# One padded table for the position terms, a pinned order in the scan's last chunk, the state turned by halves, and the last spectral rows in two loads

## The chip, the cores and the metric

The kernel runs on one core of a Trainium2 chip. What counts is the device time of one execution in microseconds (us). Three executions of the kernel before took 3838.72, 3837.66 and 3835.54 us; their median is 3837.66 us. A further execution, with the hardware profiler on, gives the profile from which everything else is read.

## The reference

The input is one image of 48x48 positions with 768 channels, in float32. Four layers follow each other:

```
x = L0(x)   # attention with relative position terms, then an MLP
x = L1(x)   # spectral layer: rfft2, block MLP per frequency, softshrink, irfft2, + x
x = L2(x)   # scan: 12 rounds of a depthwise 3x3 convolution on a state
x = L3(x)   # spectral layer as L1, other weights
```

In layer 0, with 12 heads of 64 channels, the scores get two terms which depend on the query and on the distance of the two positions:

```
coords = arange(H)[:, None] - arange(H)[None, :] + (H - 1)
Rh = rel_pos_h[coords];  Rw = rel_pos_w[coords]          # rel_pos_*: (95, 64)
rel_h = einsum('bhwc,hkc->bhwk', q, Rh)
rel_w = einsum('bhwc,wkc->bhwk', q, Rw)
attn  = softmax(attn + rel_h[..., :, None] + rel_w[..., None, :])
```

For one row (or column) of queries the factor is thus a window of 48 columns of the same table of 95 columns, shifted by one from row to row. In layer 2, `rope` turns pairs of channels by an angle:

```
for i in range(12):
    inj  = rope(silu(x @ W_B + ...), theta * (i + 1)) * silu(x @ W_X + b_X)
    H    = alpha * (conv3x3(H) + conv_b) + [gamma *] inj [+ (1 - gamma) * alpha * prev]
    prev = inj
out = silu((rope(C, theta * 12) * H) @ W_out + b_out)
```

In layer 3 the inverse transform ends with the sum over the 25 kept column frequencies, real and imaginary parts, for each row of the image; the layer's input is added.

## The kernel before, in words

A Python function writes the program; a scheduler then places the instructions of each engine, and tile pools decide when a buffer is free. `V` is VectorE (DVE), `nc.scalar` is ScalarE (ACT), `GP` is GpSimd (POOL), `nc.tensor` is TensorE (PE), and most loads and stores are issued on SyncE (SP, `nc.sync`). A float32 matmul shows as two records of PE with a weight load each. The stages stand in time like this: query, key and value products (`qkv_phase`) to 479 us and their tail to 512, attention to 1690, projection to 1832, MLP to 2840, first spectral layer to 3060, projections of the scan to 3232, scan rounds 3244 to 3487, its output product to 3598, and the last spectral layer to the end.

**Position terms (`position_terms` in `qkv_phase`).** The tokens are worked on in three blocks `sb` of 768. For each block there are 24 steps, 12 `rel_h` (L415) and 12 `rel_w` (L401). A step makes four positions. For each it multiplies the queries of a pair of heads (128 rows, 64 to a head) with a block-diagonal matrix of 128x96: two copies of the window, one for each head, zeros elsewhere. These matrices are made on the host (`relD`) and loaded by `tables` (L376 to L380), 192 KB to a step, into four buffers, up to three steps ahead. The result, 96 rows in one PSUM tile, is split into three bf16 parts by `split` (L366 to L374: two copies on ACT, two subtractions on DVE) and stored at the end of each set (`store`, L390). `advance` runs one step. `between` calls it after the value products (L164), and `q_and_k` calls it between the query and key products (L295), so that the steps lie singly among full 128x128 products; what is left over follows at the end, where a matmul on the maxima (`bound`, L475) also decides which form of attention runs. `ahead(1)` issues the first loads of attention.

**Attention**, not touched, runs per round a score product on two 64x128 tiles (L559), the position terms added as a bf16 product of 120 rows (L567) and the product with the values on two 128x64 tiles (L588).

**Scan, first part.** The tokens come in 8 chunks (`q`, 0 to 7), on 112 partitions. For each chunk three products of PE (L1094) make injection `g`, `x`, angle `th`, `al` and `ga`; DVE adds the bias (L1096); ACT takes Silu and Sigmoid; `sincos` makes sine and cosine of the angle and of 12 times it; `turn` (L1279, six operations of DVE) turns `g` by the angle into `i0`; H, the first state, is `i0 + ac` (L1142). After this come the sums `s0` and `s1` for the rounds, from `u = by_gamma(...)` (ACT, L1119) at L1148 to L1154. **Rounds:** eight groups of eight channels, 11 rounds, 88 groups. A group is 32 matmuls (L1183: two tiles of 128x48 each, accumulated) into one of four PSUM tiles `c0` to `c3`, two operations of DVE (L1185, L1187), a product on POOL (L1191), a copy on ACT (L1192) and one more DVE operation (L1203). In the last round the state is multiplied with the turned C instead (L1209, into `s`; the last group on DVE, the others on POOL). **Output:** `hg` holds 24 position pairs with 256 channels. For each two pairs four transposes (L1254: two pairs, two halves `j` of the channels), a copy on ACT (L1256) and the output product (L1263, two halves of the channels accumulated).

**Last spectral layer.** `spectrum_mix` runs its items (two halves of the channels, five groups `kc` of five column frequencies, four channel blocks) through four stages; the last, `s_ifft_h` (L1503), fills `us`, which is stored to `yu` with the group's last block (L1510). The final part reads the rows of `yu` back: `load` takes one of the six row groups `g` of a half (L1524, all 112 rows, 672 KB, four buffers), and `back` multiplies them with `iw` (L1682), adds the input on DVE (L1684) and stores the output (L1688). `beside` places loads and products of half 0 during the mix; half 1 is loaded after the mix.

## Time and profile before

| what | us |
|---|---|
| median of three executions | 3837.66 |
| profiled execution, its own time | 3841.45 |
| its span, first to last instruction | 3839.7 |
| rh, L415 MATMUL: 288 records of 352 ns mean | 55.8 busy |
| rw, L401 MATMUL: 288 records of 264 ns mean | 32.1 busy |
| c, L1183 MATMUL: 5632 records of 247 ns mean | 242.2 busy |

The mean granted clock of TensorE is 0.986 of full speed. A row of the waits names an instruction that kept PE idle, what released it, the time in total, how often, and the longest. "issue" stands for a wait which the profile can't put down to anything. Busy times of PE overlap, because matmuls are pipelined; the time a matmul takes in the stream is the distance from its start to the next one's. A row of the timeline has the start in us from the span's first instruction, the length in us, engine, line, operation, output and inputs, the size of the tile of the array (rows*columns), the form of the operands, and how many such instructions the row stands for.

### The profile page before, as it was taken

The numbers are of one execution on the slowest core, as the hardware profiler recorded it, in microseconds if no ns is written. First come the engines' busy times: TensorE is split into PE (matmuls) and PEld (weight loads), VectorE is DVE, ScalarE is ACT, GpSimd is POOL, SyncE is SP. The second block draws the span as 40 slices with busy tenths as digits, with TensorE's granted clock in tenths as the row PEclk, the third lists the DMA queues.
The fourth block names the chain that finished last, engine by engine and source line by source line (L and its number), as shares of the span: only waits on it lengthen the run. The fifth ranks groups of instructions, "written<-read, shape, count | busy, mean of one in ns | idle before, by whom it ended". The sixth has DMA issues, their size and how long they took to land.

```text
span 3839.7 us, 54414 instructions
## 1 busy us (share of the span) xinstructions
PE 3727.7 (97%) x22018; PEld 2255.4 (59%) x22018; DVE 2057.3 (54%) x3184; ACT 1142.8 (30%) x1908; POOL 656.5 (17%) x498
## 2 busy tenths in 40 slices
PE   7999979999999999999999999999999998999998
PEld 4666544444444444445555555555568876996685
DVE  6655456666666666555524332323325567995455
ACT  1323234444444444420310120012013356222341
POOL 3101001111111111015000000000013311981131
PEclk9999989999999999999999999999999999999999
DMA  7656563333232322124434534443454312112345
GB/s 254 211 193 194 178 184 119 113 107 128 84 112 75 115 74 91 42 71 139 151 104 136 173 107 121 133 137 104 125 166 105 108 36 93 40 33 73 97 114 155
DMA packets 266762, 460.43 MB, mean 120 GB/s; under 512 B 32941, under 2 KB 219301, under 8 KB 260007
## 3 DMA queue, kind: packets, MB, share of 16 engines
q1 hardware_dynamic: 256695, 435.93, 37.0%
q10 hardware_dynamic: 9808, 20.94, 1.5%
q8 instruction: 175, 2.87, 0.3%
q14 instruction: 84, 0.69, 0.1%
HBM read 318.49 MB, written 138.31 MB: 119 GB/s over the span
## 4 chain that ended last, share of the span: by engine, by line
PE 93%; DVE 2%; DMA 2%; issue 1%; ACT 1%; POOL 1%; SPq 0%; DVEq 0%; ACTq 0%; POOLq 0%
PE p L867 13%; PE p L930 12%; PE s L559 12%; PE av L588 12%; PE c L1183 6%; PE s L567 6%; PE qk L295 6%; PE c L1094 4%; PE v L164 3%; PE pj L164 2%; PE f_z L1489 2%; PE f_z L1488 2%; PE f_x L1453 2%; PE so L1263 2%; PE f_u L1503 2%; PE rh L415 1%
## 5 line engine op out<-in xcount | busy, mean ns | idle before, releaser
L577 DVE TENSOR_TENSOR acc<-acc,p 128x768 f32<-128x768 f32 x576 | 584.1, 1014 | 355.1 <-ACT p L569 317.1
L569 ACT ACTIVATE p<-s 128x768 f32<-128x768 f32 x648 | 478.6, 812 | 693.7 <-PE s L567 581.2
L930 PE MATMUL p<-w,h 128*128 128x384 f32 x1512 | 492.7, 486 | 0.0
L559 PE MATMUL s<-qt,kv 64*128 64x384 f32 x2592 | 478.5, 501 | 9.9 <-ACT p L569 7.7
L588 PE MATMUL av<-p,kv 128*64 128x384 f32 x2592 | 464.5, 493 | 0.0
L930 PEld LDWEIGHTS p<-w,h 128*128 128x128 f32 x1512 | 286.1, 190 | 196.9
L559 PEld LDWEIGHTS s<-qt,kv 64*128 64x128 f32 x2592 | 233.1, 187 | 250.6 <-ACT p L569 116.3
L588 PEld LDWEIGHTS av<-p,kv 128*64 128x64 f32 x2592 | 170.0, 136 | 225.2 <-issue 215.2
L867 PE MATMUL p<-x2nT,w 128*128 128x384 f32 x864 | 294.2, 490 | 3.4 <-issue 3.4
L295 PE MATMUL qk<-xnT,wqk 128*128 128x384 f32 x756 | 251.8, 490 | 5.3 <-DMA wqk<-wqk_d 5.3
L1183 PE MATMUL c<-H,bands 128*48 128x96 f32 x5632 | 242.2, 247 | 12.4 <-issue 12.4
L567 PE MATMUL s<-bt,oneh 120*128 120x384 bf16 x1296 | 249.1, 329 | 0.0
L1183 PEld LDWEIGHTS c<-H,bands 128*48 128x48 f32 x5632 | 234.6, 123 | 20.2 <-issue 12.7
L867 PEld LDWEIGHTS p<-x2nT,w 128*128 128x128 f32 x864 | 165.5, 192 | 119.5 <-issue 6.3
L867 PE MATMUL p<-xT,w 128*128 128x384 f32 x648 | 220.7, 486 | 0.0
L567 PEld LDWEIGHTS <-oneh 120*128 120x128 bf16 x1296 | 109.3, 98 | 174.6 <-issue 116.1
L295 PEld LDWEIGHTS qk<-xnT,wqk 128*128 128x128 f32 x756 | 144.3, 192 | 99.6 <-issue 7.9
L906 POOL TENSOR_TENSOR rr<-rr,ml_b 128x1152 f32<-128x1152 f32 x12 | 31.9, 2661 | 957.6 <-DMA rr<-xr_d 677.5
L862 ACT ACTIVATE h<-h,ml_b 128x384 f32<-128x384 f32 x144 | 88.3, 615 | 346.8 <-DVE h L882 174.3
L1191 POOL TENSOR_TENSOR t<-s,c 128x768 f32<-128x768 f32 x80 | 144.6, 1831 | 178.7 <-DVE s L1154 167.6
L867 PEld LDWEIGHTS p<-xT,w 128*128 128x128 f32 x648 | 123.1, 190 | 85.9
L597 DVE RECIPROCAL rec<-rs 128x384 f32<-128x384 f32 x36 | 92.1, 2558 | 100.6 <-PE rs L595 100.6
(323 smaller groups left out, 4800.6 us busy)
## 6 DMA issues: line engine op xcount, KB each, us to landing
w<-w1s_d SPq DMA_DIRECT2D x36, 768.0 KB
w<-w2s_d SPq DMA_DIRECT2D x36, 768.0 KB
bt<-rh_d SPq DMA_DIRECT2D x144, 162.0 KB
w<-w1s_d SPq DMA_DIRECT2D x36, 576.0 KB
w<-in_mlp_w_dram SPq DMA_DIRECT2D x27, 768.0 KB
wqk<-wqk_d SPq DMA_DIRECT2D x12, 1344.0 KB
yu<-f_ys SPq DMA_DIRECT2D x24, 672.0 KB
f_gt<-yu SPq DMA_DIRECT2D x24, 672.0 KB
```

The costliest lines, as they stand in the source:

```text
L164: nc.tensor.matmul(p[:, :TB], lhsT=rhs[n][:, c, t * P : (t + 1) * P], rhs=w[:, c, :], start=c == 0, stop=c == NC2 - 1)
L295: nc.tensor.matmul(p[:, :TB], lhsT=w[:, n, c, :], rhs=ops[sb][n][:, c, :], start=c == 0, stop=c == NC2 - 1)
L559: nc.tensor.matmul(ps[:, s, :QB], lhsT=keys[pr % 2][rows, kt * P : (kt + 1) * P], rhs=qbs[qc % 2][0][rows], start=True, stop=False)
L567: nc.tensor.matmul(ps[:, s, :QB], lhsT=oneh[:NBR, b % 3, :], rhs=qbs[qc % 2][1][:NBR, s, b // 3, j, :], start=False, stop=True)
L569: nc.scalar.activation(p, ps[:, :, :QB], AF.Exp)
L577: nc.vector.tensor_tensor(probs[c], probs[c], p, ALU.add)
L588: nc.tensor.matmul(avs[c][rows, :QB], lhsT=vals[pr % 2][:, kt, rows], rhs=p[:, s, :], start=kt == 0, stop=kt == NT - 1)
L867: nc.tensor.matmul(p[:, :TB], lhsT=w[n][:, c, :], rhs=rhs[n][:, c, :], start=c == 0, stop=c == NC2 - 1)
L930: nc.tensor.matmul(ps[t][:, :TB], lhsT=hs[left, f][:, t * P : (t + 1) * P], rhs=wt[:, f % KW2, :], start=f == 0, stop=f == NF2 - 1)
L1094: nc.tensor.matmul(ps[:K, i, :n], lhsT=v[:, c, tok : tok + K], rhs=w[:, cc, c0 : c0 + n], start=cc == NC - 1, stop=cc == 0)
L1183: nc.tensor.matmul(ps[r0 : r0 + G, k // 4, cols], lhsT=bands[:, n - GC, i, :] if gr else bands0[:, n, i, :], rhs=H[:, n, :, d : d + NPR], ...
L1191: GP.tensor_tensor(t, sc[:, ch], c1[:, m0 : m0 + GC].unsqueeze(2).to_broadcast([P, GC, RR, NPR]), ALU.mult)
```

## The change

Four places are edited.

1. *Position terms.* The table `relT` of 95 columns, which was on chip already for the bound, gets 16 columns of zeros behind each half, so that each window of 64 columns lies inside it. `terms` makes two matmuls to a position, one for each head, with 64 rows and 64 columns each; head 0 gives PSUM rows 0 to 47 and head 1 rows 64 to 111 (the rows behind them hold what nobody reads). `split` takes 128 rows. `relD`, its loads and the list of steps loaded ahead are gone. Six of the steps left over now run ahead of the maxima, the others after `ahead(1)`.

```diff
-            rel = qp.tile([P, 2, 2 * G - 1], F32, tag="rel", name="rel")
+
+            rel = qp.tile([P, 2, G - 1 + HD], F32, tag="rel", name="rel")
+            V.memset(rel[:, :, 2 * G - 1 :], 0.0)
             for s in range(2):
-                nc.sync.dma_start(rel[s * HD : (s + 1) * HD], relT)
+                nc.sync.dma_start(rel[s * HD : (s + 1) * HD, :, : 2 * G - 1], relT)
...
-            def tables(which, g, n):
-
-                d = qp.tile([P, 4, R], F32, tag="relD", name=f"relD_{which}_{g}_{n}", bufs=4)
-                nc.sync.dma_start(d, rel_d[which, g])
-                return d
+            def terms(which, pos, out, rhs):
+
+                for s in range(2):
+                    rows = slice(s * HD, (s + 1) * HD)
+                    nc.tensor.matmul(out[rows], lhsT=rel[rows, which, G - 1 - pos : G - 1 - pos + HD], rhs=rhs[rows], start=True, stop=True)
...
-                        nc.sync.dma_start(d[s, :, :, sb, cols], at[s * G : (s + 1) * G].rearrange("k n c b t -> k n (c b t)"))
+                        nc.sync.dma_start(d[s, :, :, sb, cols], at[s * HD : s * HD + G].rearrange("k n c b t -> k n (c b t)"))
...
-                    d, at = tiles.pop(("w", g)), tiles["rw"]
+                    at = tiles["rw"]
...
                     for i in range(4):
-                        nc.tensor.matmul(pv[:, :, :, i, :], lhsT=d[:, i, :], rhs=q6[:, :, :, j, w0 + i, :], start=True, stop=True)
+                        terms(1, 4 * g + i, pv[:, :, :, i, :], q6[:, :, :, j, w0 + i, :])
...
-                    d, at = tiles.pop(("h", cp, n, hh)), tiles["rh"]
+                    at = tiles["rh"]
...
                     for i in range(4):
                         rhs = q6[:, 2 * cp : 2 * cp + 2, n, :, :, 4 * hh + i].rearrange("p c j w -> p c (j w)")
-                        nc.tensor.matmul(ps[:R, i * 2 * G : (i + 1) * 2 * G], lhsT=d[:, i, :], rhs=rhs, start=True, stop=True)
+                        terms(0, 4 * (2 * (2 * sb + n) + hh) + i, ps[:, i * 2 * G : (i + 1) * 2 * G], rhs)
...
-                def load(key, *args):
-                    tiles[key] = tables(*args, "_".join(str(k) for k in (sb, *key)))
...
-                            key = "h", cp, n, hh
-                            steps.append((lambda key=key: load(key, 0, 2 * (2 * sb + key[2]) + key[3]), lambda key=key: rel_h(*key[1:])))
+                            steps.append(lambda args=(cp, n, hh): rel_h(*args))
                 for g in range(G // 4):
-                    steps.append((lambda g=g: load(("w", g), 1, g), lambda g=g: rel_w(g)))
-
-            steps, ready = [], []
+                    steps.append(lambda g=g: rel_w(g))
...
             def advance():
-                while len(ready) < 3 and steps:
-                    load, run = steps.pop(0)
-                    load()
-                    ready.append(run)
-                if ready:
-                    ready.pop(0)()
+                if steps:
+                    steps.pop(0)()
...
                 q_and_k(sb, lambda q: position_terms(sb, q), advance)
+            for _ in range(6):
+                advance()
...
             mx = qp.tile([1, 1], F32, tag="mx", name="mx")
             V.tensor_reduce(mx, ps[:1, : 2 * NC], axis=AX.X, op=ALU.max)
             V.tensor_scalar(flag, mx, SAFE, None, ALU.is_lt)
-            for _ in range(4):
-                advance()
             inner.close()
-            for _ in range(5):
-                advance()
             ahead(1)
-            while steps or ready:
+            while steps:
                 advance()
```

2. *Scan chunks.* The order in which the operations are written is changed for all chunks: angle and sines ahead of the bias of `g`, then Silu of `x`, `g`, `c`, both Sigmoids, `turn`, `ac` and H, and only then the sines of 12 times the angle and what the rounds need. For the last chunk (`q == NQ - 1`), marked instructions are kept in program order by `tc.keep_in_program_order`.

```diff
-                        for i, (z, c0, n) in enumerate(parts):
-                            V.tensor_tensor(z[:, :, t], ps[:K, i, :n], bias[:K, c0 : c0 + n], ALU.add)
+                        biased = [lambda z=z, c0=c0, n=n, i=i, t=t, ps=ps: V.tensor_tensor(z[:, :, t], ps[:K, i, :n], bias[:K, c0 : c0 + n], ALU.add) for i, (z, c0, n) in enumerate(parts)]
+                        biased.pop(0)()
+                        if t < R4 - 1:
+                            biased.pop(0)()
                     g3 = g.rearrange("p (n r) t -> p n r t", r=RR)
                     c, x = za[:, :NCR, :], za[:, NA - 1 - RR : NA - 1, :]
...
                     alq = al[:K, :, prs]
-                    for t in (g, x):
-                        nc.scalar.activation(t, t, AF.Silu)
                     th = temp([NM * R4], "th", q)
                     V.tensor_copy(th, thz.rearrange("p m t -> p (m t)"))
                     cs = sincos(th, q, "t1")
-                    V.tensor_scalar(th, th, float(ITERS), None, ALU.mult)
+
+                    pin = tc.keep_in_program_order if q == NQ - 1 else lambda ins: ins
+                    pin(biased.pop(0)())
+                    for t in (x, g, c):
+                        pin(nc.scalar.activation(t, t, AF.Silu))
+
+                    V.tensor_tensor(g.rearrange("p (n r) t -> p n (r t)", r=RR), g.rearrange("p (n r) t -> p n (r t)", r=RR), x.rearrange("p r t -> p (r t)").unsqueeze(1).to_broadcast([K, NN, RR * R4]), ALU.mult)
+                    pin(nc.scalar.activation(alq, za[:, NCR : NCR + NN, :], AF.Sigmoid))
+                    pin(nc.scalar.activation(ga, za[:, NA - 1 : NA, :], AF.Sigmoid))
+                    i0 = temp([NCR, R4], "i0", q)
+                    i03 = i0.rearrange("p (n r) t -> p n r t", r=RR)
+                    m = [temp([NM, RR, R4], f"m{j}", q) for j in range(2)]
+                    for op in turn(V, i0, g, over_r(cs[:, 0], NM), over_r(cs[:, 1], NM), m):
+                        op()
+
+                    ac = temp([NN, R4], "ac", q)
+                    V.tensor_tensor(ac, alq, cb[:K].unsqueeze(2).to_broadcast([K, NN, R4]), ALU.mult)
+                    V.tensor_tensor(H[:K, :, :, 1 + q * R4 : 1 + (q + 1) * R4], i03, over_r(ac, NN), ALU.add)
+                    pin(V.tensor_scalar(th, th, float(ITERS), None, ALU.mult))
                     cs12 = sincos(th, q, "t12")
-                    nc.scalar.activation(c, c, AF.Silu)
-                    nc.scalar.activation(ga, za[:, NA - 1 : NA, :], AF.Sigmoid)
-                    nc.scalar.activation(alq, za[:, NCR : NCR + NN, :], AF.Sigmoid)
                     nc.sync.dma_start(c_d[:K, q, :NCR], c)
                     nc.sync.dma_start(c_d[:K, q, NCR:].rearrange("p (s m) t -> p s m t", s=2), cs12)
                     c1q = c1[:K, :, prs]
-                    V.tensor_scalar(c1q, cs[:, 0], 2.0, None, ALU.mult)
+                    pin(V.tensor_scalar(c1q, cs[:, 0], 2.0, None, ALU.mult))
 
...
                     om = temp([1, R4], "om", q)
-                    V.tensor_scalar(om, ga, -1.0, 1.0, ALU.mult, ALU.add)
+                    pin(V.tensor_scalar(om, ga, -1.0, 1.0, ALU.mult, ALU.add))
...
-                    ac = temp([NN, R4], "ac", q)
-                    V.tensor_tensor(ac, alq, cb[:K].unsqueeze(2).to_broadcast([K, NN, R4]), ALU.mult)
...
-                    V.tensor_tensor(H[:K, :, :, 1 + q * R4 : 1 + (q + 1) * R4], i03, over_r(ac, NN), ALU.add)
```

3. *The state turned by halves.* All transposes of the first half of the channels (groups 0 to 3) are issued first, four pairs to a PSUM tile; those of the second half then go among the output products.

```diff
-            hTs = []
+            hTs = {}
+
+            def turned(j, q4):
+
+                ps = pt.tile([P, 512], F32, tag="t", name=f"ht_{j}_{q4}")
+                for t in range(4):
+                    nc.tensor.transpose(ps[:, t * P : t * P + K], hg[:K, 4 * q4 + t, j * P : (j + 1) * P], ident[:K, :K])
+                hTs[j, q4] = tp.tile([P, 4, 2, G], F32, tag=f"hT{j}_{q4}", name=f"hT_{j}_{q4}", bufs=1)
+                nc.scalar.copy(hTs[j, q4], ps.rearrange("p (i s w) -> p i s w", i=4, s=2)[:, :, :, :G])
...
+            for q4 in range(NPR // 4):
+                turned(0, q4)
             for half in range(2):
                 cols = slice(half * TB, (half + 1) * TB)
                 for p2 in range(NPR // 2):
-                    if half == 0:
-                        ps = pt.tile([P, 512], F32, tag="t", name=f"ht_{p2}")
-                        for t in range(2):
-                            for j in range(2):
-                                nc.tensor.transpose(ps[:, (2 * t + j) * P : (2 * t + j) * P + K], hg[:K, 2 * p2 + t, j * P : (j + 1) * P], ident[:K, :K])
-                        hT = tp.tile([P, 4, 2, G], F32, tag=f"hT{p2}", name=f"hT_{p2}", bufs=1)
-                        nc.scalar.copy(hT, ps.rearrange("p (i s w) -> p i s w", i=4, s=2)[:, :, :, :G])
-                        hTs.append(hT)
-                    hT = hTs[p2]
+                    if half == 0 and p2 % 2 == 0:
+                        turned(1, p2 // 2)
...
                         for j in range(2):
-                            nc.tensor.matmul(ps[:BS, :TB], lhsT=hT[:, 2 * t + j].rearrange("p s w -> p (s w)"), rhs=wo[:, j, cols], start=j == 0, stop=j == 1)
+                            nc.tensor.matmul(ps[:BS, :TB], lhsT=hTs[j, pr // 4][:, pr % 4].rearrange("p s w -> p (s w)"), rhs=wo[:, j, cols], start=j == 0, stop=j == 1)
```

4. *Last spectral rows.* The last group's store of the last half is issued in two parts of 192 columns. Rows 0 to 79 (`most`, the first four frequency groups) of half 1 are loaded without waiting for it, for g = 0 to 2 during the mix; rows 80 to 111 (`rest`) follow. There are five buffers instead of four.

```diff
-            if b == HB - 1:
-                nc.sync.dma_start(yu[half][4 * KC * kc : 4 * KC * (kc + 1)].rearrange("(k q) p c -> (q p) k c", q=4), us)
+            last = kc == NKC - 1 and half == halves[-1]
+            if b == HB - 1 or (last and b == HB // 2 - 1):
+                done = slice(b // 2 * 2 * BS, (b + 1) * BS) if last else slice(0, TB)
+                nc.sync.dma_start(yu[half][4 * KC * kc : 4 * KC * (kc + 1), :, done].rearrange("(k q) p c -> (q p) k c", q=4), us[:, :, done])
...
-        def load(half, g):
-            gts[half, g] = load_spectrum(nc, bp, yu, half, g, "f3", 4)
+        def load(half, g, rows=slice(0, YR)):
+            if (half, g) not in gts:
+                gts[half, g] = bp.tile([YR, 4, TB], F32, tag="gt", name=f"f3_gt_{half}_{g}", bufs=5)
+            nc.sync.dma_start(gts[half, g][rows], yu[half][rows, 4 * g : 4 * g + 4, :])
...
         items = 2 * NKC * (NB // 2)
-        loads = {items - 13 + 2 * g: g for g in range(4)}
+        loads = {items - 13 + 2 * g: g for g in range(NTB)}
         backs = {items - 8: 0, items - 5: 1, items - 2: 2, items: 3, items + 1: 4, items + 2: 5}
+
+        most, rest = slice(0, 4 * KC * (NKC - 1)), slice(4 * KC * (NKC - 1), YR)
 
         def beside(step):
             if step in loads:
                 load(0, loads[step])
             if step in backs:
-                g = backs[step]
-                back(0, g)
-                if g + 4 < NTB:
-                    load(0, g + 4)
+                back(0, backs[step])
+            if items <= step < items + 3:
+                load(1, step - items, most)
 
         spectrum_mix(tc, "f3", opened, yu, psum, False, "left", (0, 1), beside)
-        for g in range(4):
-            load(1, g)
+        for g in range(NTB - 1):
+            if g > 2:
+                load(1, g, most)
+            load(1, g, rest)
         for g in range(NTB):
             back(1, g)
-            if g + 4 < NTB:
-                load(1, g + 4)
+            if g == 0:
+                load(1, NTB - 1)
```

## The prediction

> **What bounds the kernel now.** I read the page first, then PE's waits, then the timeline of PE around each place the diff touches. Two lines of the page (busy time of an engine with its share of the span; the chain that ended last, by engine):
>
> ```profile
> PE 3727.7 (97%) x22018; PEld 2255.4 (59%) x22018; DVE 2057.3 (54%) x3184; ACT 1142.8 (30%) x1908; POOL 656.5 (17%) x498
> ...
> PE 93%; DVE 2%; DMA 2%; issue 1%; ACT 1%; POOL 1%; SPq 0%; DVEq 0%; ACTq 0%; POOLq 0%
> ```
>
> TensorE is the bound nearly everywhere: what adds to its stream is paid in full, and what can be won is its 112 us of idle time. The waits of PE (operation and line, releaser, us in total, times, longest):
>
> ```profile
> PE n_tp L93 <- DVE x L84: 18.3, 3, 11.5
> PE c L1183 <- issue: 12.4, 1, 12.4
> PE f_w L1682 <- DMA f_gt<-yu: 11.8, 1, 11.8
> PE rw L401 <- DMA relD_w<-in_relD_dram: 9.6, 3, 6.2
> ...
> PE ht L1254 <- DVE s L1209: 5.9, 1, 5.9
> PE qk L295 <- DMA wqk<-wqk_d: 5.3, 1, 5.3
> PE bound L475 <- DVE pz L471: 3.4, 1, 3.4
> ...
> PE ht L1254 <- DVE H L1187: 2.2, 1, 2.2
> PE s L559 <- DVE rest_w L372: 2.1, 1, 2.1
> ```
>
> Each part of the change aims at one of them: tables (rw, part of qk), scan start (c L1183, really the DVE and ACT work before H), turned state (ht), last rows (f_w). They hold 9.6 + 12.4 + 8.1 + 11.8 = 41.9 us, and none can go entirely. Next, position terms among v matmuls (start, us, engine, operation, tile rows*columns, count):
>
> ```profile
> 176.76 2.12 PE L164 MATMUL v<-wv,xnT 128*128 128x384 f32 x6
> 178.71 1.56 PE L415 MATMUL rh<-q,relD_h 128*96 128x96 f32 x8
> 180.10 2.12 PE L164 MATMUL v<-wv,xnT 128*128 128x384 f32 x6
> 182.05 0.84 PE L401 MATMUL rw<-q,relD_w 128*96 128x96 f32 x8
> 182.73 2.13 PE L164 MATMUL v<-wv,xnT 128*128 128x384 f32 x6
> ```
>
> By starts, an rh step of four matmuls (two records each) takes 1.39 us, an rw step 0.68. Between 70 and 185 us PE is busy 115.00 of 115.00 us, between 336 and 380 it is 43.96 of 44: such a step has no slack beside it. Last, an attention round, the only place where this trace changes tile shapes:
>
> ```profile
> 522.06 2.21 PE L559 MATMUL s<-qt,kv 64*128 64x384 f32 x12
> 524.20 1.15 PE L567 MATMUL s<-bt,oneh 120*128 120x384 bf16 x6
> 525.28 2.16 PE L588 MATMUL av<-p,kv 128*64 128x384 f32 x12
> 527.36 2.21 PE L559 MATMUL s<-qt,kv 64*128 64x384 f32 x12
> ```
>
> [...] The twelve s records are six pairs whose single records start 7 ns apart, 0.322 us from pair to pair, as for a full array; six pairs make 1.93 us, but the s block takes 2.14 (522.06 to 524.20), the av block 2.08. The single records split this surplus: about 0.10 is the drain at the end of each block (last start to first start 0.415 us instead of 0.316), the rest is the first pair's weight load, which can't be fetched ahead: 0.104 for 128 columns, 0.052 for 64. [...]
>
> **A, position terms.** Removed: 72 loads of 192 KB on SP's queue and 288 matmuls on 128x96 tiles. Added: 576 on 64x64 tiles, in pairs (rows 0 to 63 and 64 to 127), and one memset, beside loads. Rate of a step: if the pairs run side by side, unchanged, 0 us; the c L1183 pairs (128x48 tiles, 96 columns) also pass at 0.086 us, the pace of rw, so issue doesn't limit it. If not, another 0.68 or 1.39 each. I take 0. The splits on DVE and ACT have 128 rows instead of 96, elements per row equal: 0.
>
> Switches: the order of the changed kernel leaves 56 of the 72 steps singly between v or qk matmuls of 128x128 (32 rh, 24 rw), the other 16 in a block at the end. Each single step pays 0.10 + 0.05 to enter and 0.10 + 0.10 to leave, 0.35 us; entering today's 128x96 costs nothing (v to rh starts 0.322 us apart, the usual pace). 56 x 0.35 = **+19.7**, all on the path. Bounds: 0 if no drain showed, 0.45 (25 us) if both weight loads of a pair showed one behind the other.
>
> The tail, from the last qk matmul (478.7) to the first s (511.61), is 32.9 us:
>
> ```profile
> 487.96 2.22 PE L401 MATMUL rw<-q,relD_w 128*96 128x96 f32 x24
> 490.62 0.89 PE L401 MATMUL rw<-q,relD_w 128*96 128x96 f32 x8 [0.44 <-DMA relD_w<-in_relD_dram]
> 494.43 3.63 PE L401 MATMUL rw<-q,relD_w 128*96 128x96 f32 x24 [2.93 <-DMA relD_w<-in_relD_dram]
> 504.28 5.18 PE L401 MATMUL rw<-q,relD_w 128*96 128x96 f32 x40 [6.22 <-DMA relD_w<-in_relD_dram]
> 511.61 1.85 PE L559 MATMUL s<-qt,kv 64*128 64x384 f32 x9 [2.15 <-DVE rest_w L372]
> ```
>
> The 9.6 us of table waits go, but DVE is late next: a step gives it two subtractions, 1.13 us start to start, and after the rh store of the step before frees the buffer (about 486 us, as now) 16 steps end at 486 + 18 = 504 to 505. So s starts near 505, 6.5 earlier; PE idles longest just before, and a cold clock takes back about 1. Taken: **-5.5**, range -3 to -9. Six steps now stand ahead of the bound matmul, with their splits ahead of the maxima on DVE; flag is read when attention begins, after the splits anyway, so nothing waits for it. On SP the first bias loads no longer stand behind ten table loads: hidden.
>
> The qk wait of 5.3 us (392 to 397): its load is issued at 380.0 behind a 1.2 MB key/value load, a 1.3 MB store and v stores, DMA 0.93 busy; only about one table load (0.2 MB, under 1 us at 275 GB/s) drops out. **-1**, range 0 to -5.3. The 18.3 us for x at L84 stay, since they lie ahead of the first table.
>
> **B, the scan's last chunk.** PE idles from 3232.2 to 3244.5. ACT has five table loads of 1.28 us there, the DVE chain waits for sines, and H is written last (3243.48 to 3244.44). After: sines first, with their table resident, g and x ahead of c, sigmoid later, and H ahead of everything only the next rounds need. Following each engine's pinned order with the durations of the trace, H ends near 3243.0: -1.5. But the second injection (u, L1119) and its sum then come at 3251.9 instead of 3249.67, and the updates of c (L1185, L1187) queue behind them on DVE: the first PSUM tile comes free near 3255.7, while PE's fourth group wants it at 3254.1. Today it had 2.0 us of slack; a stall of 1.7 follows, not made up, because DVE at 2.7 to 2.8 us a group is no faster than PE at 2.753. Sum **+0.25**, range -1.5 to +3.
>
> **C, the state by halves.** Today one transpose runs at 3488.92, then PE waits 5.88 us for the last state group, then come 47 transposes at 0.116 and the so matmuls, the first 16 records cold in 7.58 us instead of 5.16. After: 24 transposes of the first half (groups 0 to 3, ready) and two half products run in that wait: 23 x 0.116 = 2.7, plus 1.3 for the products, plus part of a 2.2 us wait and the cold clock, less weight not hidden: **-4.5**, range -3 to -6. ACT's copies keep their number of elements.
>
> **D, the last spectral rows.** Today the last store is issued at 3804.77 (5.4 us), the load at 3810.26, and PE starts at 3815.82. After: the store goes as two halves, rows 0 to 79 come earlier, and only 32 rows (197 KB) follow the second half. Most bytes now stand in front of that half: outputs 590 KB twice, loads 492 KB twice, halves 369 KB twice, 2.9 MB at about 275 KB/us, so it lands near 3811.5 and the rows near 3814.4: **-1.4**, range -5.5 to +1. SP's half store also waits behind a load whose buffer frees at 3803.2; included.
>
> Sum: +19.7 - 5.5 - 1 + 0.25 - 4.5 - 1.4 = **+7.6 us**. The profiled execution took 3841.45 us (span 3839.7 and 1.75 around it), 3.8 above the median of 3837.66. So 3849 in such an execution and 3845 against the median. A difference under 0.2%, 7.7 us, can't be told from none here: the sum lies on that line.
>
> **Rivals.** (1) Cheap switches. Place: the 56 single steps. Break-even is 12.15 / 56 = 0.217 us a step, since the rest gains 12.15. If the weights of the next shape load during the drain, 0.19 remains (3836); if 64x64 drains nothing visible, 0 (3825.5). Middle, 3831: faster or the same. For it: v to rh today shows no cost. Against it: every shape change of attention shows 0.10 and an exposed load. (2) The halves of a pair run one behind the other[...]. Then 32 x 1.39 + 24 x 0.68 = 61 us come on top: 3906. [...] (3) The tail gives nothing, because attention's start is held by the key/value and bias loads, or by the split chain restarting at a later store: 3845 + 5.5 = 3851. For it: DMA moved up to 338 GB/s there; against it: ten loads fewer.
>
> **How the numbers follow.** Chances: forecast 0.47 (own range 3836 to 3855), cheap switches 0.28 (3823 to 3836), serial pairs 0.12, tail without gain 0.13. Faster by over 0.2% (under 3830): 0.19 of the second case and 0.07 of the first, 0.26. Slower (over 3845.3): 0.18 of the forecast, 0.11 of the tail case, 0.12 of serial pairs, 0.41. Same: 0.33. The range 3822 to 3868 leaves out serial pairs and some of the gains' far end.
>
> **What would show it.** Starts between a v matmul and the first term after it near 0.47 us instead of 0.32, and v after the terms later by 0.20; the first record of the pair within 10 ns of the second (rival 2: 85 to 175 ns later); no table waits and s near 505; the first c at about 3243 and a wait of 1 to 2 us some groups later; an ht wait under 2 us; f_w's wait near 10. A switch under 0.2 us or pairs in series make the prediction wrong.

## The result, and the profile after

| | before | after |
|---|---|---|
| median | 3838.19 us (3835.54 to 3841.08, 4 runs) | 3861.62 us (3860.10 to 3862.20, 4 runs) |
| profiled execution, its span | 3841.45, 3839.7 | 3861.23, 3859.3 |
| bytes moved by DMA | 460.43 MB | 446.35 MB |
| TensorE matmul records | 22018 | 22594 |

The ratio is 1.0059, 95% interval 1.0047 to 1.0072: the changed kernel is 23.4 us slower. Its trace has what the change says: 576 more records, and 14.1 MB less, which is the 72 table loads of 192 KB.

The waits of PE in the kernel after (operation and line, releaser, us in total, times, longest):

```profile
PE n_tp L93 <- DVE x L84: 17.9, 3, 10.5
PE qk L295 <- DMA wqk<-wqk_d: 14.2, 2, 14.0
PE c L1177 <- issue: 10.9, 1, 10.9
PE f_w L1685 <- DMA f_gt<-yu: 8.8, 1, 8.8
PE s L549 <- ACT p L559: 8.4, 2, 7.0
...
PE ht L1246 <- ACT hT L1248: 6.5, 1, 6.5
PE s L549 <- DVE rest_w L372: 5.7, 1, 5.7
```

The table waits (9.6 us) are gone. The scan's first convolution waits 10.9 instead of 12.4, the last rows 8.8 instead of 11.8. But the wait for the q and k weights grew from 5.3 to 14.0 in one place, and the turned state still waits 6.5, for another engine. So of the four aims the last rows were met, the turned state hardly, and the other two were met and paid for elsewhere: the tables in this stage, the scan's start in the rounds behind it.

A ledger shows where the time came from. The same matmul is found in both traces, and the difference of its start times is the loss up to there. Where the difference jumps, time is lost or won:

| from the start up to | loss so far, us | what lies in the step |
|---|---|---|
| the long qk wait of the last block | +12.3 | most of the shape switches, +15.1; the start and the order of work, -2.8 |
| just behind that wait | +21.5 | the wait itself, +8.7, and a slower pace right behind it, +0.5 |
| last qk matmul | +24.0 | the other switches, +2.6 |
| first attention score s | +19.3 | the tail, -4.7 |
| first av | +21.6 | the first s block at a granted clock of 0.50, +2.3 |
| first spectral matmul | +22.3 | the loads behind the last store, +0.7 |
| end of the scan's projection | +21.2 | -1.1 |
| first convolution of the scan | +19.7 | H earlier, -1.5 |
| last convolution | +22.8 | the rounds, +3.1 |
| last output product | +20.9 | the turned state, -2.0 |
| last f_u of the last layer | +23.6 | +2.7, scatter (see the end of this part) |
| end | +19.6 | the last rows, -4.0 |

First, the switches. The timeline of PE in the kernel after (start, us, engine, line, operation, tile rows*columns, shape, count):

```profile
175.51 2.20 PE L164 MATMUL v<-wv,xnT 128*128 128x384 f32 x6
177.65 1.59 PE L380 MATMUL rh<-q,rel 64*64 64x96 f32 x16
179.17 2.20 PE L164 MATMUL v<-wv,xnT 128*128 128x384 f32 x6
...
182.83 2.20 PE L164 MATMUL v<-wv,xnT 128*128 128x384 f32 x6
184.96 0.88 PE L380 MATMUL rw<-q,rel 64*64 64x96 f32 x16
185.77 2.20 PE L164 MATMUL v<-wv,xnT 128*128 128x384 f32 x6
```

From one v block to the next it is 3.66 us over an rh step and 2.94 over an rw step (179.17 - 175.51, 185.77 - 182.83). Before, the same distances were 3.34 and 2.63. So a step that stands alone costs 0.32 us more, and 56 of them 17.7. The two records of a pair start 6 to 7 ns apart, and pairs pass at 0.175 and 0.083 us, as the wider matmuls did: the halves run side by side.

Second, the qk wait, in the kernel before and then after:

```profile
378.38 13.71 PE L295 MATMUL qk<-xnT,wqk 128*128 128x384 f32 x42
397.37 4.18 PE L295 MATMUL qk<-xnT,wqk 128*128 128x384 f32 x6 [5.28 <-DMA wqk<-wqk_d]
```

```profile
390.69 13.71 PE L295 MATMUL qk<-xnT,wqk 128*128 128x384 f32 x42
418.39 2.90 PE L295 MATMUL qk<-xnT,wqk 128*128 128x384 f32 x4 [13.99 <-DMA wqk<-wqk_d]
```

Why that load came late is read from SP's queue in the kernel after (start and length of each issue):

```profile
385.88 0.57 SPq L505 DMA_DIRECT2D kv<-v_d  x1
386.54 2.98 SPq L390 DMA_DIRECT2D rw_d<-rw  x2
389.57 4.03 SPq L234 DMA_DIRECT2D v_d<-v_o  x1
393.70 3.85 SPq L245 DMA_DIRECT2D wqk<-wqk_d  x1
```

The order is that of before, where the load was issued at 380.04 and PE went on at 397.37: 17.3 us. Now it is issued at 393.70 and PE goes on at 418.39: 24.7 us. The issue moved by 13.7 us and PE's work by 12.3, so most of the loss, 7.4 us, lies between issue and landing. In front of the load stand a store of position terms (`rw_d<-rw`, two transfers of 1296 KB, one per head) and a store of values. The store's packets can be told by their size of 9216 bytes. The windows from its first packet to its last, before and then after (from:to, length, busy time and instructions of PE, PEld, DVE, ACT, POOL, then PE's clock, the share of the 16 DMA engines that is busy, GB/s):

```profile
377.70:389.80 12.10, 12.10 (x39) 7.16 (x38) 3.09 (x6) 1.71 (x3) 2.61 (x1) 1.00 1.01 283
```

```profile
391.20:410.70 19.50, 13.20 (x41) 7.41 (x40) 5.87 (x10) 2.94 (x5) 2.61 (x1) 0.90 0.97 248
```

The DMA engines are full in both, yet the same store takes 12.1 us before and 19.5 after. From its last packet to PE's next record it is 7.5 us before and 7.7 after, so the 7.4 us are those of the store. In the packet records the first head's packets (the first 144 of 288 in order of their start) take 544 ns before and 552 after; the second head's 518 before and 834 after. Only the second head's source changed: it lies in rows 48 to 95 before, in rows 64 to 111 after. This store was in the diff (`at[s * HD : s * HD + G]` for `at[s * G : (s + 1) * G]`) and is what the experiments turned to.

Third, the start of attention after. The second fence gives windows over it, columns as above:

```profile
522.26 1.54 PE L380 MATMUL rw<-q,rel 64*64 64x96 f32 x32 [1.20 <-DVE rest_w L372]
524.33 0.88 PE L380 MATMUL rw<-q,rel 64*64 64x96 f32 x16 [0.54 <-DVE rest_w L372]
530.91 4.21 PE L549 MATMUL s<-qt,kv 64*128 64x384 f32 x12 [5.71 <-DVE rest_w L372]
```

```profile
526.00:531.00 5.00, 0.09 (x2) 0.12 (x2) 4.27 (x9) 2.42 (x5) 0.00 (x0) 0.86 0.00 0
531.00:535.10 4.10, 4.10 (x13) 1.96 (x14) 0.56 (x1) 0.04 (x1) 0.00 (x0) 0.50 0.63 128
```

PE is idle for 5.71 us while DVE ends the splits, and the granted clock is 0.50 right behind it: the first 12 s records take 4.21 us, where before, at a clock of 1.00, they took 2.21.

The third layer's +2.7 us is not read as an effect of the change: from the last output product to the last f_u it took 205.7 to 208.7 us over all traces of this study, 205.7 before and 207.2 in an experiment whose code there is that of before. It also means that the two profiled executions (19.8 us apart) hold the 23.4 us of the medians only to a few us.

### The profile page after: what moved, and what is told of

Same layout as the page of the kernel before. It is cut to its first block, busy times and chain, and to the rows that moved or that the text cites. A ratio compares the mean times of both kernels' runs of the same rounds, so it can differ in the third digit from the quotient of the medians.

```text
span 3859.3 us, 55411 instructions
## 1 busy us (share of the span) xinstructions
PE 3746.5 (97%) x22594; PEld 2242.5 (58%) x22594; DVE 2056.5 (53%) x3185; ACT 1148.2 (30%) x1911; POOL 652.1 (17%) x498
## 2 busy tenths in 40 slices
DMA packets 257598, 446.35 MB, mean 116 GB/s; under 512 B 32157, under 2 KB 210133, under 8 KB 250839
## 4 chain that ended last, share of the span: by engine, by line
PE 86%; DVE 5%; DMA 4%; ACT 2%; issue 1%; POOL 1%; SPq 1%; ACTq 0%; DVEq 0%; POOLq 0%
PE p L857 13%; PE p L920 13%; PE s L549 12%; PE av L578 11%; PE s L557 6%; PE qk L295 6%; PE c L1084 4%; PE v L164 3%; PE f_z L1487 2%; PE f_z L1488 2%; PE pj L164 2%; PE f_x L1452 2%; PE f_u L1502 2%; PE so L1262 2%; DVE s L1197 2%; DVE H L1181 1%
## 5 line engine op out<-in xcount | busy, mean ns | idle before, releaser
L549 PE MATMUL s<-qt,kv 64*128 64x384 f32 x2592 | 480.5, 503 | 14.1 <-ACT p L559 8.4
L1177 PE MATMUL c<-H,bands 128*48 128x96 f32 x5632 | 244.1, 247 | 12.2 <-issue 10.9
L1177 PEld LDWEIGHTS c<-H,bands 128*48 128x48 f32 x5632 | 234.2, 123 | 22.3 <-issue 11.3
```

The lines of the kernel that those rows point to most:

```text
L549: nc.tensor.matmul(ps[:, s, :QB], lhsT=keys[pr % 2][rows, kt * P : (kt + 1) * P], rhs=qbs[qc % 2][0][rows], start=True, stop=False)
L1177: nc.tensor.matmul(ps[r0 : r0 + G, k // 4, cols], lhsT=bands[:, n - GC, i, :] if gr else bands0[:, n, i, :], rhs=H[:, n, :, d : d + NPR], ...
```

## The experiments

The parts of the change are called as in the prediction: A the position terms, B the scan's last chunk, C the turned state, D the last spectral rows. Runs that were sent together are compared with the same runs of the kernel before, whose median was 3839.5 to 3839.7 us each time. The changed kernel was timed in the first comparison only, beside a kernel before of 3838.19, so a difference of medians against it is known to 1 or 2 us only. Twelve kernels were run.

**The parts alone.** The first took A back and left B, C and D: the hunks of the diff in the attention's projection were undone, with the matching store.

> The changed kernel with the position terms as before (tables by DMA, one 128x96 matmul to a position); the scan order, the turned state and the last rows stay changed. Theory (the position terms carry the loss: 56 single steps at 0.32 us, and a qk wait of 14 us): 3836 to 3839 us, no switch cost, the qk wait back near 5.3 us. Rival (the scan's stalls and the third layer's wait carry most): 3845 us or more.

It took 3837.66 us (3834.65 to 3840.06, 13 runs), ratio 0.9995 (0.9986 to 1.0003). So A carries the whole loss, 24 us; what B, C and D win together can't be told from nothing.

**Whose bytes delay the weights?** One suspect was the first load of values (`kv<-v_d`), which the changed kernel issues just ahead of the store. It was made to wait for a later instruction:

```diff
-                    ahead(0)
+                    ahead(0, kt)
...
+            nc.vector.tensor_copy(kvs[0][:1, T : T + 1], gate[:1, 0, :1])
```

> The changed kernel, where the first load of values (kv<-v_d, 1.2 MB) waits for a result of the second pair of query and key products, so that it can't stand ahead of the second wqk load. Theory (these bytes ahead of the wqk load make the wait): the qk wait falls from 14 to under 4 us, 3848 to 3852 us. Rival (the wait comes from the stores with rows at 64 to 111, or from a slow spell of memory): it stays over 8 us, 3857 us or more.

3855.21 us (3853.41 to 3858.37), 1.0043 (1.0029 to 1.0056): the time lies between the two expectations, the qk wait of 8.2 us just on the rival's side. The load of values in front accounts for some 6 us of the 14. The weights were now issued at 388.64 instead of 393.70, but the store took 20.4 us from first packet to last, its two halves 718 and 818 ns a packet, so the cause was still there.

**What does a switch cost?** Two steps were put behind each other, so that there are 28 places instead of 56:

```diff
-                    if pr > 1 and n in (2, 5):
+                    if pr > 1 and n == 5:
+                        step()
                         step()
...
-                for _ in range(-(-left // slots[0])):
-                    advance()
+                if slots[0] % 2 == 0:
+                    for _ in range(2 * -(-left // slots[0])):
+                        advance()
```

> The changed kernel with the single steps put two behind each other, in 28 places instead of 56; same matmuls. Theory (the cost is paid per place, for changing the tile shape there and back, 0.32 us): 28 x 0.32 = 9 us less, 3852 to 3854 us. Rival (it is paid per step, for the weights of 64x64 pairs): no more than 2 us less, 3859 us or more.

3844.41 us (3840.27 to 3847.12, 21 runs), 1.0013 (1.0006 to 1.0019). Its timeline:

```profile
184.19 1.54 PE L381 MATMUL rw<-q,rel 64*64 64x96 f32 x32
185.66 4.14 PE L164 MATMUL v<-wv,xnT 128*128 128x384 f32 x12
189.73 1.54 PE L381 MATMUL rw<-q,rel 64*64 64x96 f32 x32
```

Two steps and twelve v records take 5.54 us (189.73 - 184.19); apart they took 2 x 2.94 = 5.88. One place less is 0.34 us here, and up to the last qk matmul the kernel won 8.5 us, the qk wait left aside, against 28 x 0.32 = 9.0 by the distances above. Another 7.5 came from the qk wait, which fell from 14.0 to 6.5: the load of values now came behind the weights in the queue. So the time lies 8 us below the theory's. The price of a switch is confirmed by its place, not by the total.

**The rows of the store.** The author's guess was that the rows which a store reads decide how long it takes. Two kernels change this one thing, in opposite directions. The changed kernel was given back rows 48 to 95 for the second store (its second head's stored terms are then partly those of other rows):

```diff
-    ... at[s * HD : s * HD + G].rearrange("k n c b t -> k n (c b t)"))
+    ... at[s * G : (s + 1) * G].rearrange("k n c b t -> k n (c b t)"))
```

> The changed kernel, but the second head's store of the position terms reads rows 48 to 95 instead of 64 to 111, as the kernel before did (its stored terms are therefore partly the wrong rows). Same bytes, same packets, same matmuls. Theory ([...]the store drains slowly[...]): mean time of a 9216-byte packet of the second store falls from 0.84 to about 0.55 us, the qk wait from 14 to 5 to 8 us, 3852 to 3856 us. Rival (the wait comes from the order or from the missing table loads): wait 12 us or more, 3859 us or more.

The kernel before was made to read rows 0 to 47 for both heads (so both heads store the first one's terms):

```diff
-    ... at[s * G : (s + 1) * G].rearrange("k n c b t -> k n (c b t)"))
+    ... at[:G].rearrange("k n c b t -> k n (c b t)"))
```

> The kernel before, but the second store reads rows 0 to 47 again instead of rows 48 to 95 (the second head's stored terms are those of the first). [...]the second store is as slow as in the changed kernel, the qk wait rises from 5 to 9 to 14 us, 3843 to 3848 us. Rival: within 2 us of the kernel before.

A third keeps the rows of the changed kernel, 0 to 47 and 64 to 111, but lets the heads take turns, each store in three parts:

```diff
-    for s in range(2):
-        nc.sync.dma_start(d[s, :, :, sb, cols], at[s * HD : s * HD + G].rearrange("k n c b t -> k n (c b t)"))
+    for n in range(3):
+        for s in range(2):
+            nc.sync.dma_start(d[s, :, n, sb, cols], at[s * HD : s * HD + G, n].rearrange("k c b t -> k (c b t)"))
```

> The changed kernel with each pair of stores issued in three parts, first and second head in turn[...]. [...]the pair drains faster than one after the other, the qk wait falls from 14 to under 8 us, 3851 to 3856 us. Rival (bytes or order alone): no more than 2 us less; more issues on SP could even cost 1 us.

The same store, at about 380 to 410 us of the span:

| kernel | rows of the second store | first packet to last | packet, first and second half of the 288 | qk wait | median |
|---|---|---|---|---|---|
| before | 48 to 95 | 12.2 us | 544, 518 ns | 5.3 | 3839.5 |
| before, rows 0 to 47 twice | 0 to 47 | 16.7 | 575, 866 | 9.3 | 3853.49 (1.0036, 1.0024 to 1.0048) |
| after | 64 to 111 | 19.5 | 552, 834 | 14.0 | 3861.62 |
| after, rows 48 to 95 | 48 to 95 | 14.3 | 558, 539 | 7.2 | 3845.58 (1.0018, 1.0011 to 1.0026) |
| after, heads in turn | 64 to 111 | 13.3 | 633, 536 | 0.3 | 3835.37 (0.9989, 0.9981 to 0.9997) |

In the first four rows of the table the two halves are taken as the two heads; with the heads in turn each half holds packets of both. The qk waits of the two kernels with other rows, first the kernel before with rows 0 to 47 twice, then the changed one with rows 48 to 95:

```profile
PE qk L295 <- DMA wqk<-wqk_d: 10.0, 2, 9.3
```

```profile
PE qk L295 <- DMA wqk<-wqk_d: 7.2, 1, 7.2
```

In both the queue has the same order as in the kernel they were made from. The rows alone move the kernel before by +14 us and the kernel after by -16, more than either expectation. The profiled execution of the second took 3850.88, 5 us above its median; against the trace of the kernel after it shows 7.5 us of the gain at the qk wait, 0.6 in the tail and 3.4 at the start of attention.

With the heads in turn, PE at the place of the qk wait:

```profile
389.82 13.71 PE L295 MATMUL qk<-xnT,wqk 128*128 128x384 f32 x42
403.86 9.59 PE L295 MATMUL qk<-xnT,wqk 128*128 128x384 f32 x29 [0.33 <-DMA wqk<-wqk_d]
```

The wait of 14.0 us is now 0.33. But this edit changed more than the turns. SP's queue there:

```profile
380.67 10.15 SPq L391 DMA_DIRECT2D rw_d<-rw  x6
...
392.74 1.68 SPq L245 DMA_DIRECT2D wqk<-wqk_d  x1
...
407.56 0.56 SPq L506 DMA_DIRECT2D kv<-v_d  x1
```

The load of values, which stood ahead of the store in the kernel after (385.88), now stands behind the weights, as in the experiment that made it wait. That one is the fair comparison: 3855.21 to 3835.37, 19.8 us for the stores in turn, with 20.4 us from first packet to last going to 13.3. The other 6 of the 26 us are those of the load of values. That the heads alternate was not separated from the finer parts either: six parts with the first head's three in front were not tried.

The second place is in attention, 41 us after its start. PE's wait of 7.0 us there is put down to ACT's `p`, which waits for a product of POOL, which waits for a load of projection weights (`pw0b`, issued on SP at 563.0; its semaphore was complete at 568.9). The load stands behind the last store and all that followed it in SP's queue. In the kernel with the heads in turn that wait is gone. PE's waits ahead of s in that kernel:

```profile
PE s L550 <- DMA rw_d<-rw: 5.7, 1, 5.7
...
PE s L550 <- ACT p L560: 1.7, 1, 1.7
```

The 1.7 us are another place, the second s block, where the kernel after waits 1.4. The third place is the tail. PE's wait ahead of the first s is 5.7 us as it was, but the tail is 2.7 us shorter; 1.5 of it is that ACT's copies of the last rh terms, which need the buffer of the store before, start 8.0 us after the last qk matmul instead of 9.5. This kernel is 26 us faster than the changed one, and 4 us faster than the kernel before.

While the second head's packets ran, all DMA together moved 277 GB/s in the kernel before (382.6 to 389.8 us, 518 ns a packet) and 235 in the kernel after (396.2 to 410.7 us, 834 ns a packet). Rows 0 to 47 are not slow in every place: the first head's packets take only 544 to 575 ns, with other transfers beside them (296 GB/s from 391.2 to 396.0 in the kernel after), and the same rows as a second store 866. That the rows decide is shown; by what means was not shown, and no run here tells one cause from another.

**The scan.** To give POOL and ACT less to do ahead of the rounds, the sines of 12 times the angle were moved to the end of each chunk:

```diff
-                    pin(V.tensor_scalar(th, th, float(ITERS), None, ALU.mult))
-                    cs12 = sincos(th, q, "t12")
-                    nc.sync.dma_start(c_d[:K, q, NCR:].rearrange("p (s m) t -> p s m t", s=2), cs12)
...
-                    gc = temp([NM * R4], "th", f"{q}_g").rearrange("p (m t) -> p m t", t=R4)
+                    gc = temp([NM, RR, R4], "m0", f"{q}_g")[:, :, 0, :]
...
+                    pin(V.tensor_scalar(th, th, float(ITERS), None, ALU.mult))
+                    cs12 = sincos(th, q, "t12")
+                    nc.sync.dma_start(c_d[:K, q, NCR:].rearrange("p (s m) t -> p s m t", s=2), cs12)
```

The angle `th` is thus needed longer, so a product that shared its buffer (`gc`) was given another.

> The changed kernel with the sines of 12 times the angle put at the end of each scan chunk, after the sums s0 and s1. Theory (the second sum comes late behind these sines and holds the first PSUM tile): the rounds' loss of 3.1 us falls under 1.2 us, H stays as early, 3859 to 3860 us, the first rounds without waits for s. Rival (DVE is simply behind in the first groups whatever the order on ACT): 3861 to 3862 us.

A miss: 3868.34 us (3863.69 to 3872.20), 1.0075 (1.0062 to 1.0089), 6.7 more than the changed kernel. The first product of the rounds on POOL, after and then in this kernel:

```profile
3273.07 5.39 POOL L1185 TENSOR_TENSOR t<-s,c 128x768 f32<-128x768 f32 x3 [169.73 <-DMA bands<-in_bands_dram]
```

```profile
3280.52 5.34 POOL L1185 TENSOR_TENSOR t<-s,c 128x768 f32<-128x768 f32 x3 [180.11 <-DMA c_d<-t]
```

It waits for the store of the late sines: the rounds' buffer appears to take the place of those sines, so the store must have read them first. PE then stands 5.56 us for its first free tile. What is needed last should not be made last if its buffer is wanted next.

**The turned state.** After the last convolution, PE, DVE and ACT in the kernel after:

```profile
3511.76 0.96 PE L1246 MATMUL ht<-ident,s 112*128 112x112 f32 x8 [2.15 <-DVE H L1181]
3519.23 1.75 PE L1246 MATMUL ht<-ident,s 112*128 112x112 f32 x8 [6.51 <-ACT hT L1248]
```

```profile
3517.12 1.47 DVE L1203 TENSOR_TENSOR s<-H,crg 112x768 f32<-112x768 f32 x1 [5.51 <-DMA crg<-cr_d]
```

```profile
3518.69 0.86 ACT L1248 COPY hT<-ht 128x384 f32<-128x384 f32 x2 [23.54 <-DVE s L1203]
```

Only 8 of the 24 transposes run early, two PSUM tiles full. Then they wait for ACT's copies, and ACT's first copy waits for the last state group on DVE (L1203), the wait that the new order was to step around. That group waits 5.51 us for its load, of which there are two buffers. Four were given:

```diff
-                        cr = tp.tile([P, NQ, GC * RR, R4], F32, tag="crg", name=f"crg_{gr}", bufs=2)
+                        cr = tp.tile([P, NQ, GC * RR, R4], F32, tag="crg", name=f"crg_{gr}", bufs=4)
```

> The changed kernel with four buffers instead of two for the turned C of the last scan round (crg), so that the load for the last state group no longer waits for a buffer. Theory (the turning stands behind the last multiplication, which waits for this load, because the copies of the turned state reuse memory of the state): the ht wait on ACT of 6.5 us falls under 2 us and the output product starts 4 to 5 us earlier, 3856 to 3858 us. Rival (what is won is given back in the third layer, whose first loads wait for their stores): output product earlier, but 3860 us or more.

PE and DVE in this kernel:

```profile
3512.37 1.61 PE L1246 MATMUL ht<-ident,s 112*128 112x112 f32 x8 [2.15 <-DVE H L1181]
3514.46 1.75 PE L1246 MATMUL ht<-ident,s 112*128 112x112 f32 x8 [0.48 <-ACT hT L1248]
```

```profile
3512.32 1.50 DVE L1203 TENSOR_TENSOR s<-H,crg 112x768 f32<-112x768 f32 x1
```

The load's wait is gone and the transposes wait 0.48 instead of 6.51 us. From the last convolution to the last output product it is 104.4 instead of 109.2 us; the median is 3854.63 (3851.90 to 3857.17), 1.0037 (1.0023 to 1.0051), 7 below the changed kernel, of which the traces show the 4.8 here. Why the copies need L1203 is inferred: the tiles of hT are opened in the memory that the scan's state H held, and L1203 is its last reader. A kernel with the copies in other memory was not tried.

**All together.** Heads in turn, two steps to a place and four buffers:

> The changed kernel with the stores in turn (as in the interleaved run), the steps two behind each other in 28 places, and four buffers for the turned C. Theory (the three costs are separate): 3835 less 28 x 0.32 = 9 less 4 to 6: 3820 to 3823 us, no wqk wait over 2 us. Rival (they overlap, so that the sum isn't reached): 3827 us or more.

3818.13 us (3816.93 to 3823.23), 0.9946 (0.9932 to 0.9960), in time as expected, though the qk wait is 3.0 us, not under 2. To see how much of this the kernel before could have had, the position terms went back to the tables, with heads in turn and four buffers:

> The position terms as before (tables by DMA, 128x96 matmuls), the stores issued in turn, four buffers for the turned C, the scan order, turned state and last rows as changed. Theory (the stores also held the kernel before: its wqk wait of 5 us and the wait for the next bias loads of 6 us): 3837.7 less 5 to 10 for the stores less 4 to 6: 3822 to 3829 us. Rival (rows 0 to 47 and 48 to 95 already drain well enough): 3831 us or more.

3821.36 us (3813.98 to 3822.10), 0.9944 (0.9930 to 0.9958), with the qk wait 3.0, and the wait in attention, which the expectation puts down to the bias loads, 1.2 instead of 6.0. So stores head by head, with the load of values in front, were costing the kernel before too (that load moved behind the weights here as well); the change made an old cost larger. With that settled, the padded table with two steps to a place no longer differs measurably from the loads. Four steps to a place, 14 places:

```diff
-                    if pr > 1 and n == 5:
-                        step()
-                        step()
+                    if pr in (3, 5) and n == 5:
+                        for _ in range(4):
+                            step()
...
-                if slots[0] % 2 == 0:
-                    for _ in range(2 * -(-left // slots[0])):
+                if slots[0] % 4 == 0:
+                    for _ in range(4 * -(-left // slots[0])):
```

> As with two steps, but four behind each other, in 14 places. Theory (paid per place): 14 x 0.32 = 4.5 us less than with two, 3815 to 3819 us. Rival (four steps fill four of six PSUM buffers, and their splits on ACT and DVE hold the products behind them): no better than with two, or slower, with waits for the splits in PE's list.

3818.76 us (3814.57 to 3822.39), 0.9947 (0.9933 to 0.9961). In the trace the last qk matmul comes 4.8 us earlier than with two steps, as 14 x 0.32 = 4.5 says, but the medians are equal: inconclusive in the total. Last, the same with the scan's chunks in the order of the kernel before:

> As with four steps, stores in turn and four buffers for the turned C, but the scan chunks in their old order. Theory (the pinned order begins 1.5 us earlier and loses 2 to 3.5 us in the first rounds): from the last projection matmul to the first round 12.4 us instead of 10.9, the rounds 242.0 us instead of 243.8 to 245.5, so 0.5 to 2 us less in all, and a median of 3817 to 3818 us. Rival (the order is a gain, and the stalls come from elsewhere): the rounds stay at 243.8 us or more, and the time rises by 1.5 us to 3820.

3816.08 us (3813.35 to 3819.27), 0.9939 (0.9926 to 0.9953). The first convolution waits 12.4 again, and the rounds take 243.65 us instead of 242.0, so the scan is 256.0 long, no longer than with the new order (254.7 to 256.4 in the ten traces that have it, the late sines left aside) and longer than the 254.3 of the two traces of the kernel before. What B is worth stays open. This kernel has the lowest median of the study, 23.6 us below the kernel before on the same chip, but its interval overlaps those of the three above.

## Why the prediction was right or wrong

The time, 3861.62, lies in the range of 3822 to 3868, 17 us above the forecast of 3845, and on the side that had the largest chance. It is outside the forecast's own 3836 to 3855, and that it lies in the wider range is in part luck: the largest loss behind the switches was not in the sum. The sum was +7.6; the medians show +23.4, the spans of the profiled executions +19.6. Of the 12 us between sum and spans, 10 are the qk wait; the other errors nearly cancel.

**The step that failed** is the qk wait: "only about one table load (0.2 MB, under 1 us at 275 GB/s) drops out. **-1**, range 0 to -5.3". It became +9.2, of which 8.7 are the wait. The step counted the bytes that leave the queue in front of the weights, and took the rate at which the rest drains as given. It also counted the store as 1.3 MB, where two such transfers stand, one for each head. The part of the change that altered the rate, the rows from which the second head's terms are stored, was not priced at all; of the 128 rows only the splits on DVE and ACT were considered, and these do keep their time: the first subtraction (L372) took 551 and 549 ns on 96 rows before, 554 and 550 on 128 after. The runs showed in its place: 48 other rows make the second head's packets take 834 ns instead of 518, and this alone is 14 to 16 us in either kernel. It works in three places, of which the qk wait is the largest. Some 6 us hang on the load of values in front of the store, which the kernel before had there too.

- **Switches, 0.35 us each, +19.7 (56 x 0.35 is 19.6).** Right: 0.32 us, 17.7 in all. The rate of a step, taken as unchanged, was right as well: pairs 6 to 7 ns apart. Rival 2, an estimate for a case that the trace before doesn't show, falls, and rival 1 too, since it needed less than 0.217.
- **The tail, -5.5.** Right in its mechanism, mis-sized: the sum had 6.5 us less about 1 for a cold clock, the runs show 4.7 less 2.3 at a granted clock of 0.50, so -2.4, outside its range of -3 to -9. DVE's splits are late next, as the sum had it. The result lies midway between forecast and rival 3, which gave the tail nothing; one of the rival's reasons, a later store, is real: in the turn-taking kernel the tail is 2.7 us shorter still.
- **First bias loads, "hidden".** True of those of the first round; what follows the last store in the queue isn't hidden: the wait in attention that hangs on it is 7.0 us instead of 6.0, and gone with the heads in turn.
- **B, +0.25.** The -1.5 for H came out (12.35 to 10.89, and 12.4 to 10.9 in the experiments). The stall behind it was predicted at 1.7 and came as two waits in the first groups, 1.3 together:

```profile
3276.79 8.13 PE L1177 MATMUL c<-H,bands 128*48 128x96 f32 x192 [0.46 <-DVE s L1197]
3285.74 14.46 PE L1177 MATMUL c<-H,bands 128*48 128x96 f32 x330 [0.82 <-DVE s L1197]
```

  But the rounds took 3.15 us longer in all. The old order in the last experiment also ran 1.7 us longer than in the kernel before, so part of this is not the order; what it is stays open.
- **C, -4.5.** Mis-sized: -2.0, and -6.8 once the last state group had its load in time (four buffers). It assumed that 24 transposes and two half products fit into the wait. Eight did, where before two (not one) had run ahead of the wait, because two PSUM tiles were full and the copies that empty them waited for the very group that was late. That "ACT's copies keep their number of elements" was true and beside the point: it was their wait that counted.
- **D, -1.4.** Mis-sized: -4.0, inside the range of -5.5 to +1. The estimate put 2.9 MB ahead of the last half store and its rows ready at 3814.4; the load of the rest was issued 5.1 us behind the half store, much as before (5.5), but PE went on 2.9 us behind that issue instead of 5.6. So 2.7 of the gain is the shorter load, and 1.0 is that the 48 matmuls behind it start over 17.3 us instead of 18.3:

```profile
3828.34 0.32 SPq L1511 DMA_DIRECT2D yu<-f_us  x1
3833.46 8.07 SPq L1677 DMA_DIRECT2D f_gt<-yu  x6
```

```profile
3836.34 13.88 PE L1685 MATMUL f_w<-f_gt,f_iw 100*96 100x384 f32 x36 [8.76 <-DMA f_gt<-yu]
```

## What to carry to other kernels

When a change moves data to other partition rows, price every transfer that reads those rows, and everything that stands behind it in its queue: here the compute was right to a few us, and a store of unchanged size cost 16. If two stores of one kind read different ranges of rows, try them in smaller parts that take turns: here that won some 20 us. And of a step that is to run in another's wait, follow its outputs too: who empties its tiles, and what that engine waits for.

## What the runs showed of the hardware that was not expected

- Stores of the same bytes and packets from 48 rows took 518 to 539 ns a packet from rows 48 to 95, 834 from rows 64 to 111 and 866 from rows 0 to 47, each behind a store from rows 0 to 47, which itself took 544 to 575; in turns, 536 to 633.
- Matmuls on two 64x64 tiles (input rows 0 to 63 and 64 to 127), a shape that the kernel before doesn't have, run side by side, 6 to 7 ns apart, with both halves in one PSUM tile.
- After 5.71 us of idle time TensorE ran its next block at a granted clock of 0.50: 4.21 us for what takes 2.21.
